# A decoder's fp8 self attention: the outputs' products in another accumulator bank, and the cross inputs' rounding at another place of the turn

## The chip, the core and the metric

The kernel is one program on one core of a Trainium2 chip. The metric is the device time of one execution in microseconds. A core has five engines that matter here, each with a queue of its own that it works through in order: TensorE (PE, matrix products, with a separate row PEld for loading its stationary operand), VectorE (DVE), ScalarE (ACT), GpSimd (POOL) and SyncE (SP, which issues nearly all DMAs). PE writes its products into eight accumulator banks (PSUM), from which DVE and ACT read them.

## What is computed

The reference is a two layer decoder on 16 sequences of 112 tokens with 512 channels. It runs in seven stages: a causal attention, an attention with fp8-rounded inputs (self and cross part), a mixture of experts, a second causal attention, a cross attention over the context, and a ternary feed-forward layer. The change lies in the self part of the second one:

```python
xq = _div_clamp_fp8(x, in_scale)          # clip to +-448, round to bf16, then to fp8 e4m3
q  = einsum('bsi,oi->bso', xq * in_scale, wq) * w_scale   # k and v alike, with scales of their own
p  = softmax(einsum('bsghd,btgd->bghst', ln(q), ln(k)) / sqrt(128))
o  = einsum('bghst,btgd->bsghd', p, v)    # then rounded to fp8 again, times wproj, added to x
```

The cross part needs the same x rounded with a fourth scale. The self stage does this rounding for it, on the side, and stores the result in DRAM.

## The kernel before

`stage_fp8_self` works on 64 units: a unit is one batch with one quarter q of the heads (four query heads, two key and value heads). Their order is fixed by `self_order`: quarters 0 and 1 are interleaved in units 0 to 31, then come quarter 2 (units 32 to 47) and quarter 3 (48 to 63). The 1792 tokens make 14 tiles of 128 rows, while a batch has 112 rows. So of eight batches, one (b = 7 or 15) has no tile of its own and hence no queries to project, and one (b = 0 or 8) finishes no tile and hence has no output product.

A software pipeline runs over turns: `turn(n)` issues one step each of several units. In the order of the code, and so of PE's queue, a turn holds the query product of unit n (`ps_q`), the scores of unit n-2 (`ps_s`), the transposes of the probabilities of unit n-3 (`ps_pt`), the key and value products of unit n (`ps_kv`), the values product of unit n-3 (`ps_av`), the transposes of queries and keys of unit n-1 (`ps_t`), and the output product of unit n-4 (`ps_acc`). PE and ACT keep the written order in all turns up to 63, DVE from turn 5 on. POOL and SP, and every engine in the last four turns (the drain), are ordered by the scheduler.

DVE's part of a turn, in order: the minimum over the scores (`su_m`), the sums of squares of the queries (`su_v`), the centring of new weights if any (`centers`), the reciprocals of the softmax sums (`su_s`), the second half of the weights' splitting (`ends`), the sums of squares of the keys, the smoothing and rounding of unit n-3's values (`smooth_fp8`, which uses `round_fp8`), the scaling of queries and keys (`qk`), the rounding of one cross tile (`quantize_cross`), and the addition of the output product to x (`x<-ps_acc`, in `add_output`). ACT computes the exponentials behind `su_m` (`pr`). POOL divides them by their sums (`pr<-pr,su_s`), subtracts weights' low halves (`w_self<-raw,w_self`), takes the power for the layer norm (`su_v`), and finishes each rounding (`r_o`, `xqx`).

`quantize_cross` runs in turns behind unit 31 in which no weights are centred, 14 times in all. It loads a tile `r_y` from `yx_dram`, rounds it with four DVE instructions (L530 to L534) and one on POOL (`xqx`), and stores it to `xx_dram`. The load and its rounding are in the same place of the same turn.

The stage divides the eight banks into pools: `mm` has three (for `ps_q` and `ps_kv`), `tr` one (for the transposes of the inputs, `ps_xt`, which end with the inputs in turn 20), `sc` four (for `ps_s`, `ps_pt`, `ps_av`, two `ps_t`, and `ps_acc`). The cross stage behind it has a bank `acc` for the same output products.

```python
tag = "acc" if "acc" in k.banks else "sc"
acc = k.psum.tile([P, D], F32, tag=tag, name="ps_acc", bufs=k.banks[tag])
```

Of the kernel before, what the change touches and what calls it, by code (L numbers as in the profile page):

```python
# [11 lines left out]
BF16 = mybir.dt.bfloat16  # L12
# [8 lines left out]
P = 128  # L21
# [4 lines left out]
KC = D // P  # L26
# [3 lines left out]
TILES = B * S // P  # L30
# [30 lines left out]
def done_tile(b):  # L61

    return tile_of(b - 1) if b % 8 else None
# [381 lines left out]
def from_positions(k, dst, src, t):  # L445

    src = src.rearrange("(s b) d -> b s d", b=B)
    for b, s, r, n in batches_of(t):
        k.nc.sync.dma_start(out=dst[r : r + n], in_=src[b, s : s + n])
# [73 lines left out]
def round_fp8(k, wk, y, parts, tag="r8"):  # L523

    nc = k.nc
    m = wk.tile(list(y.shape), BF16, tag=f"{tag}_m", name="r8_m", bufs=2)
    t = wk.tile(list(y.shape), BF16, tag=f"{tag}_t", name="r8_t", bufs=2)
    nc.vector.tensor_scalar(y, y, FP8_MAX, -FP8_MAX, ALU.min, ALU.max)  # L530
    nc.vector.tensor_scalar(m.bitcast(U16), y.bitcast(U16), 0x7F80, None, ALU.bitwise_and)
    nc.vector.tensor_scalar(m, m, 2.0**-6, 1.5 * 2.0**4, ALU.max, ALU.mult)

    nc.vector.tensor_tensor(t, y, m, ALU.add)  # L534
    for dst, tok in parts:
        nc.gpsimd.tensor_tensor(dst, t[:, :, tok], m[:, :, tok], ALU.subtract)  # L536
# [153 lines left out]
def two_parts(k, out, lhs, w, first=True, last=True):  # L690

    n = w[0].shape[1]
    for c in range(n):
        for i in range(2):
            k.nc.tensor.matmul(  # L695
                out, lhs(c), w[i][:, c, :], start=first and c == 0 and i == 0,
                stop=last and c == n - 1 and i == 1,
            )
# [55 lines left out]
def quantized(k, wk, b, xv):  # L754

    xq, t = None, tile_of(b)
    if t is not None:
        xq = wk.tile([P, 2, KC, P], F32R, tag="xq", name="xq", bufs=3)
        k.nc.sync.dma_start(out=xq.bitcast(F32), in_=k.xq_dram[t])
    xv[b] = wk.tile([P, KC, S], F32R, tag="xv", name="xv", bufs=4)  # L760
    k.last_load = k.nc.sync.dma_start(out=xv[b].bitcast(F32), in_=k.xv_dram[b])
    return xq


def quantize_cross(k, wk, t):

    y = wk.tile([P, KC, P], BF16, tag="r8_y", name="r8_y", bufs=2)
    k.nc.sync.dma_start(out=y, in_=k.yx_dram[t])
    xq = wk.tile([P, 2 * KC, P], BF16, tag="y_0", name="xqx", bufs=1)
    xq = xq.rearrange("p c s -> p (c s)").bitcast(F32).rearrange("p (c s) -> p c s", c=KC)  # L770
    round_fp8(k, wk, y, [(xq, slice(0, P))])
    k.nc.sync.dma_start(out=k.xx_dram[t], in_=xq)
# [10 lines left out]
class SelfUnit:  # L783
# [108 lines left out]
            )  # L892
        smooth_fp8(k, wk, av, 4 * self.q, self.b, self.heads.o)

    def output(self):
        t = done_tile(self.b)
        if t is not None:
            add_output(self.k, t, self.heads.o.pop(t), self.w.get(3))


def to_batches(k, wk, dst, ps, t, tag, cols):
# [20 lines left out]
    round_fp8(k, wk, y, parts)  # L922


def add_output(k, t, o, w):

    tag = "acc" if "acc" in k.banks else "sc"
    acc = k.psum.tile([P, D], F32, tag=tag, name="ps_acc", bufs=k.banks[tag])
    two_parts(k, acc, lambda h: o[:, h, :], w)
    x = k.x[:, t, :]  # L930
    k.nc.vector.scalar_tensor_tensor(x, acc, k.c_proj, x, ALU.mult, ALU.add)


def self_order():


    order, then = [], 0
    for b in range(B):
        order.append((0, b))
        while then < (b - 7) * 11 // 8:  # L940
            order.append((1, then))
            then += 1
    order += [(1, b) for b in range(then, B)]
    return order + [(q, b) for q in (2, 3) for b in range(B)]


def stage_fp8_self(k):

    nc = k.nc
    with k.stage("s2a", mm=3, tr=1, sc=4) as wk:
        order = self_order()
        total = len(order)
        heads, xv = [Heads() for _ in range(4)], [{} for _ in range(4)]
        units = [SelfUnit(k, wk, q, b, heads[q]) for q, b in order]
        inputs = {
            n: Quantized(k, wk, units[n].tile, xv[0])
            for n, (q, b) in enumerate(order) if q == 0 and units[n].tile is not None
        }  # L960
        weights = k.next_w + [Weights(k, "self", q, wk, raw=2) for q in (1, 2, 3)]
        weights.append(Weights(k, "cross", 0, wk, raw=2))
        last = [order.index((q, B - 1)) for q in range(4)]

        def at(n):
            return units[n] if 0 <= n < total else None


        early = {-2: 4, -1: 1, 0: 2, 1: 2, 2: 3, 3: 2, 4: 2}
        then = list(range(B))  # L970

        def products(count):
            for b in then[:count]:
                if b % GB == 2 and b // GB + 2 < NB:
                    k.early.load(b // GB + 2)
                k.early.product(b)
            del then[:count]

        def due(n):

            if n >= 3:
                yield weights[1], 2, 3
            for q in range(3):

                if n >= last[q]:
                    yield weights[q + 2], 2 if q == 0 else 1, 3 if n >= last[q] + 4 else 1 + (q < 2)

        tiles = list(range(TILES))

        def turn(n):  # L990
            new, half = inputs.get(n + 2), inputs.get(n + 1)
            products(early.get(n, 0))
            if at(n):
                units[n].project_q(weights[order[n][0]], xq.pop(n))
            if at(n - 2):
                units[n - 2].scores()
            if at(n):
                units[n].query_sums()
            if half:
                half.round_qk()  # L1000
                xq[n + 1] = half.xq
            centered = [w.centers() for w in weights]
            if at(n - 3):
                units[n - 3].transpose_probs()
            if at(n - 2):
                units[n - 2].exponentials()
            for w in weights:
                w.ends()
            if half:
                half.scale(6)  # L1010
            if at(n):
                units[n].project_kv(xv[order[n][0]].pop(order[n][1]))
            for w, count, pieces in due(n):
                w.begin(count, pieces)
            if at(n - 3):
                units[n - 3].values()
            if at(n):
                units[n].normalize()
            if half:
                half.round_v()  # L1020
            if n > last[1] and tiles and not any(centered):
                quantize_cross(k, wk, tiles.pop(0))
            if at(n - 1):
                units[n - 1].transpose()
            if new:
                new.transpose()
                new.scale(10)
            elif at(n + 2):
                q, b = order[n + 2]
                xq[n + 2] = quantized(k, wk, b, xv[q]) if q else None  # L1030
            if at(n - 4):
                units[n - 4].output()
            if n + 3 in inputs:
                inputs[n + 3].load()
            if 0 <= n < TILES:
                from_positions(k, k.x[:, n], k.x_dram, n)

        xq = {}
        inputs[0].load()
        fixed = {mybir.EngineType.PE, mybir.EngineType.Activation}  # L1040
        with k.tc.manual_schedule(engines=fixed):
            for n in range(-2, 5):
                turn(n)
        with k.tc.manual_schedule(engines=fixed | {mybir.EngineType.DVE}):
            for n in range(5, total):
                turn(n)
        for n in range(total, total + 4):
            turn(n)
        k.next_w = weights[-1]
# [10 lines left out]
class CrossUnit:  # L1060
# [111 lines left out]
    def output(self):  # L1172
        t = done_tile(self.b)
        if t is not None:
            add_output(self.k, t, self.heads.o.pop(t), self.w.get(1))


def stage_fp8_cross(k):
# [607 lines left out]
def stage_ffn(k):  # L1786
# [66 lines left out]

STAGES = (
    stage_attn0, stage_fp8_self, stage_fp8_cross, stage_moe, stage_attn1,
    stage_cross1, stage_ffn,
)
# [147 lines left out]
```

## Time and profile before

| | us |
|---|---|
| median of three runs | 3847.8 (3841.57 to 3852.76) |
| the profiled execution | 3842.72 |
| its span in the trace | 3841.0 |
| TensorE busy, granted clock over the span | 3627.2, 0.975 |
| self stage: rounding turns, first and second stretch | 695.4 to 785 and 828 to 867 |
| the four DVE instructions of one cross rounding | 0.29, 0.29, 0.29, 0.43 |
| POOL xqx, median | 1.158 |
| exponentials of one unit, chain of waits | 1.46 |
| x<-ps_acc on DVE, median | 0.745 |

A page shows one profiled execution. Where a row names a line such as L695, it is that of kernel.py. A count such as x14 says how often. In the view of waits a line has the waiting engine and instruction, then what it waited for, then the total, the number of waits and the longest in microseconds. In the timeline a row has its start, its duration, the engine, the line, what it writes and reads, and in square brackets how long the engine sat idle before it and who ended that.

### The profile page before, as it was taken

The numbers are of one execution on the slowest core, as the hardware profiler recorded it, in microseconds if no ns is written. First come the engines' busy times: TensorE is split into PE (matmuls) and PEld (weight loads), VectorE is DVE, ScalarE is ACT, GpSimd is POOL, SyncE is SP. The second block draws the span as 40 slices with busy tenths as digits, with TensorE's granted clock in tenths as the row PEclk, the third lists the DMA queues.
The fourth block names the chain that finished last, engine by engine and source line by source line (L and its number), as shares of the span: only waits on it lengthen the run. The fifth ranks groups of instructions, "written<-read, shape, count | busy, mean of one in ns | idle before, by whom it ended". The sixth has DMA issues, their size and how long they took to land.

```text
span 3841.0 us, 46297 instructions
## 1 busy us (share of the span) xinstructions
PE 3627.2 (94%) x16482; PEld 2338.3 (61%) x16482; DVE 1764.6 (46%) x3872; ACT 1437.4 (37%) x4149; POOL 926.1 (24%) x1314
## 2 busy tenths in 40 slices
PE   7888898899899999999999999999989999999999
PEld 4455787787555566656666654555544445556788
DVE  4445777776544544544445543111243343214333
ACT  2455675554444444444444430111123341112222
POOL 2333555553322322222222210000132220000000
PEclk8999899999999999999999999999989999999999
DMA  2125333432211211211121113999830022222000
GB/s 78 52 101 172 113 101 120 132 128 79 76 51 52 76 52 46 71 49 52 42 84 49 44 47 121 314 320 317 298 129 12 1 71 82 72 74 81 11 12 17
DMA packets 118117, 364.56 MB, mean 95 GB/s; under 512 B 13280, under 2 KB 33248, under 8 KB 108848
## 3 DMA queue, kind: packets, MB, share of 16 engines
q1 hardware_dynamic: 105504, 332.20, 26.7%
q0 software_dynamic: 5040, 16.52, 1.2%
q10 hardware_dynamic: 7344, 12.89, 0.9%
q8 instruction: 131, 2.15, 0.2%
q14 instruction: 98, 0.80, 0.1%
HBM read 317.09 MB, written 44.47 MB: 94 GB/s over the span
## 4 chain that ended last, share of the span: by engine, by line
PE 69%; DVE 8%; POOL 5%; DMA 3%; issue 2%; ACT 2%; SPq 0%; POOLq 0%; ACTq 0%; DVEq 0%
PE ps_kv L1113 14%; PE ps L1470 5%; PE ps_av L1166 4%; PE ps_s L1141 3%; PE ps_y L1488 3%; PE ps_q L695 3%; PE ps_acc L695 3%; PE ps_u L1832 3%; PE ps_o L350 3%; PE ps_o L1814 3%; PE ps_g L1832 3%; PE ps_q L1583 3%; PE ps_p L1676 3%; PE ps_pt L1156 2%; PE ps_v L1598 1%
## 5 line engine op out<-in xcount | busy, mean ns | idle before, releaser
L1113 PE MATMUL ps_kv<-w_kv,ct 128*125 128x512 f32 x1408 | 638.3, 593 | 0.0
L1113 PEld LDWEIGHTS ps_kv<-w_kv,ct 128*125 128x125 f32 x1408 | 260.5, 188 | 276.1 <-issue 242.0
L536 POOL TENSOR_TENSOR r_o<-r_t,r_m 128x64 fp32r<-128x64 bf16 (+6 forms) x224 | 146.6, 671 | 326.6 <-DVE r_t L534 302.9
L1057 ACT ACTIVATE pr<-ps_s,ex_m 112x375 f32<-112x375 f32 (+1 forms) x272 | 157.4, 579 | 164.6 <-DVE ex_m L1056 154.1
L1089 DVE TENSOR_REDUCE cu_v<-sq 125x2 f32<-125x256 f32 (+1 forms) x248 | 118.6, 478 | 217.5 <-ACT sq L1088 217.5
L1470 PE MATMUL ps<-w_expert,xgt 128*128 128x448 f32 x560 | 216.4, 539 | 0.7 <-ACT xgt L1462 0.7
L517 POOL TENSOR_SCALAR cu_v<-cu_v 125x2 f32<-125x2 f32 (+1 forms) x248 | 48.0, 194 | 635.9 <-DVE cu_v L1089 633.6
L236 POOL TENSOR_TENSOR pr<-pr,nq_s 112x448 f32<-112x448 f32 (+1 forms) x120 | 119.4, 996 | 320.2 <-DVE nq_s L235 266.0
L518 POOL TENSOR_TENSOR cu_v<-cu_v,mhalf 125x2 f32<-125x2 f32 (+1 forms) x248 | 190.0, 766 | 20.4
L231 ACT ACTIVATE pr<-ps_s,nq_m 112x112 f32<-112x112 f32 (+1 forms) x480 | 167.2, 376 | 52.5 <-DVE nq_m L223 48.6
L1141 PE MATMUL ps_s<-kt,qt 128*112 128x375 f32 x512 | 183.5, 479 | 1.7 <-ACT pr L1057 1.3
L1056 DVE TENSOR_REDUCE ex_m<-ps_s 112x1 f32<-112x375 f32 (+1 forms) x272 | 148.2, 545 | 69.1 <-PE ps_s L1703 68.0
L1088 ACT ACTIVATE sq<-ps_kv 125x256 f32<-125x256 f32 x176 | 67.4, 383 | 272.8 <-PE ps_kv L1113 218.5
L511 ACT ACTIVATE qt<-ps_t,turned 128x448 f32<-128x448 f32 (+6 forms) x224 | 116.5, 581 | 130.4 <-PE ps_t L1125 121.8
L1166 PE MATMUL ps_av<-pt,vn 125*128 125x224 f32 x768 | 160.8, 358 | 0.0
L1470 PEld LDWEIGHTS ps<-w_expert,xgt 128*128 128x128 f32 x560 | 103.6, 190 | 92.0 <-issue 91.0
L1156 PEld LDWEIGHTS ps_pt<-ident,pr 112*125 112x125 f32 x768 | 104.5, 190 | 86.3 <-DVE pr L1148 48.8
L1141 PEld LDWEIGHTS ps_s<-kt,qt 128*112 128x112 f32 x512 | 89.9, 177 | 100.8 <-issue 59.1
L245 ACT COPY ptt<-ps_pt 112x448 f32<-112x448 f32 (+1 forms) x120 | 66.8, 565 | 223.0 <-PE ps_pt L243 223.0
L1156 PE MATMUL ps_pt<-ident,pr 112*125 112x112 f32 x768 | 119.8, 285 | 30.9 <-DVE pr L1148 29.0
L1166 PEld LDWEIGHTS ps_av<-pt,vn 125*128 125x128 f32 x768 | 143.5, 192 | 8.7 <-ACT pt L1159 4.6
L511 ACT ACTIVATE kt<-ps_t,vec 128x375 f32<-128x375 f32 (+7 forms) x240 | 131.4, 588 | 26.0 <-PE ps_t L1131 22.0
(294 smaller groups left out, 7377.4 us busy)
## 6 DMA issues: line engine op xcount, KB each, us to landing
w_expert<-in_moe_w SPq DMA_DIRECT2D x105, 896.0 KB
ct<-in_ctx_t SPq DMA_DIRECT2D x64, 750.0 KB
xq<-xq_dram SPq DMA_DIRECT2D x42, 512.0 KB
xq<-xx_dram SPq DMA_DIRECT2D x56, 256.0 KB
raw<-in_self_w SPq DMA_DIRECT2D x48, 256.0 KB
w_sum<-in_ffn_w SPq DMA_DIRECT2D x12, 1024.0 KB
cn<-in_ctx SPq DMA_DIRECT2D x16, 750.0 KB
xv<-xv_dram SPq DMA_DIRECT2D x48, 224.0 KB
```

What stands on the lines that cost most here:

```text
L231: nc.scalar.activation(pr[:, j, :], self.ps[:, j, r * t : (r + 1) * t], AF.Exp, bias=self.mx[r][:, j : j + 1], scale=-1.0, accum_out=sums[ ...
L511: k.nc.scalar.activation(dst, src, AF.Identity, bias=cols[:, 1:2], scale=cols[:, 0:1])
L518: nc.gpsimd.tensor_tensor(dst, dst, bc(k.minus_half[: dst.shape[0]], [dst.shape[0], n]), ALU.pow)
L695: k.nc.tensor.matmul(out, lhs(c), w[i][:, c, :], start=first and c == 0 and i == 0, stop=last and c == n - 1 and i == 1,)
L1056: nc.vector.tensor_reduce(mx, src, AX.X, ALU.min)
L1057: nc.scalar.activation(dst, src, AF.Exp, bias=mx, scale=-1.0, accum_out=sums)
L1113: nc.tensor.matmul(pkv, self.ct[:, c, ch * CC : (ch + 1) * CC], w[:, c, :], start=c == 0, stop=c == KC - 1,)
L1141: nc.tensor.matmul(ps, self.heads.qt[self.b][:, h, :], self.kt[:, h // 2, :], start=True, stop=True)
L1156: nc.tensor.transpose(ps[:, h, :], self.pr[:, h, ch * CC : (ch + 1) * CC], k.ident[:S, :S])
L1166: nc.tensor.matmul(av[:, 2 * g : 2 * g + 2, :], self.vn[:, ch, g, :], self.pt[:, ch, 2 * g : 2 * g + 2, :], start=ch == 0, stop=ch == NCH - 1,
L1470: nc.tensor.matmul(pp, self.xt[:, c, :], w[:, c, :], start=c == 0, stop=c == 3)
L1832: nc.tensor.matmul(pp, w[:, c, cols], xt[:, part, c, :], start=c == 0 and part == 0, stop=c == 3 and part == 1,)
```

## The change

There are three edits.

1. `add_output` is told its bank by its caller. In the self stage this is `sc` up to the turn of the last input (turn 22), and `tr` from then on. The cross stage goes on using `acc`.
2. The load of a cross tile is a function of its own, `cross_input`. It stands where load and rounding stood, and is issued from turn 31 on whenever no loaded tile is pending. Its buffer is the one called `y_2`, which the inputs' values used before (one buffer), where `r_y` shared two with `smooth_fp8`.
3. The rounding of the tile loaded in the turn before stands behind `centers`, so on DVE behind `su_m` and the sums of the queries and ahead of `su_s`. On POOL its `xqx` then comes ahead of the same turn's `pr`. The turns in which a tile is rounded are the same 14.

```diff
-def quantize_cross(k, wk, t):
-
-    y = wk.tile([P, KC, P], BF16, tag="r8_y", name="r8_y", bufs=2)
+def cross_input(k, wk, t):
+
+    y = wk.tile([P, KC, P], BF16, tag="y_2", name="yx", bufs=1)
     k.nc.sync.dma_start(out=y, in_=k.yx_dram[t])
+    return y
+
+
+def quantize_cross(k, wk, t, y):
+
     xq = wk.tile([P, 2 * KC, P], BF16, tag="y_0", name="xqx", bufs=1)
...
-def add_output(k, t, o, w):
-
-    tag = "acc" if "acc" in k.banks else "sc"
+def add_output(k, t, o, w, tag):
+
     acc = k.psum.tile([P, D], F32, tag=tag, name="ps_acc", bufs=k.banks[tag])
...
-        tiles = list(range(TILES))
+        tiles, loaded = list(range(TILES)), []
+        end = max(inputs)
...
             centered = [w.centers() for w in weights]
+
+            if loaded and not any(centered):
+                quantize_cross(k, wk, *loaded.pop())
             if at(n - 3):
...
-            if n > last[1] and tiles and not any(centered):
-                quantize_cross(k, wk, tiles.pop(0))
+            if n >= last[1] and tiles and not loaded:
+                loaded.append((tiles[0], cross_input(k, wk, tiles.pop(0))))
...
-                units[n - 4].output()
+
+                units[n - 4].output("sc" if n <= end else "tr")
```

## The prediction

> **What bounds the kernel now.** First the page, to see which engine the program is against. TensorE is busy for 94% of the span.
>
> ```profile
> span 3841.0 us, 46297 instructions
> ...
> PE 3627.2 (94%) x16482; PEld 2338.3 (61%) x16482; DVE 1764.6 (46%) x3872; ACT 1437.4 (37%) x4149; POOL 926.1 (24%) x1314
> ```
>
> That is an average over seven stages. The change lives in one, the fp8 self attention, so second the table of busy time for its last part: the turns that round cross inputs (first and third row), those between them (second), and the rest.
>
> ```profile
> 695.40:785.00 89.60, 77.25 (x491) 67.99 (x490) 66.59 (x157) 47.23 (x159) 49.12 (x58) 0.98 0.44 144
> 785.00:828.00 43.00, 39.91 (x259) 35.06 (x258) 35.79 (x84) 25.00 (x81) 23.33 (x28) 1.00 0.37 119
> 828.00:867.00 39.00, 35.40 (x210) 31.60 (x211) 27.25 (x62) 18.63 (x62) 22.34 (x27) 0.87 0.35 112
> 867.00:934.00 67.00, 62.76 (x396) 55.15 (x395) 45.09 (x103) 36.05 (x127) 29.14 (x39) 1.00 0.22 70
> ```
>
> The columns are the length, then PE, PEld, DVE, ACT and POOL busy, and the granted clock. In the first row PE misses 12.4 us of 89.6; in the third it misses 3.6 and ran at a clock of 0.87. Third, who waits there (waits from 690 to 935):
>
> ```profile
> POOL pr L875 <- DVE su_s L874: 73.0, 26, 4.7
> ACT pr L870 <- POOL xqx L536: 23.8, 9, 4.1
> PEld ps_acc L695 <- issue: 12.3, 8, 1.9
> PE ps_acc L695 <- ACT pr L870: 10.0, 6, 1.7
> DVE r_y L530 <- DMA r_y<-yx_dram: 4.4, 8, 0.9
> ```
>
> The second line names POOL, but the built program makes those exponentials wait for su_m on VectorE; su_m ends at 724.13 and xqx at 724.19 in the same turn, so the view picked the later of two. Fourth, the chain of waits from 716 to 738, one turn:
>
> ```profile
> 718.64 2.87 DMA r_y<-yx_dram
> ...
> 723.02 1.17 POOL xqx L536
> 724.23 1.46 ACT pr L870 x8
> ...
> 726.04 0.93 POOL pr L875
> 726.97 1.25 POOL w_self L641
> ```
>
> and three rows of the timeline:
>
> ```profile
> 723.52 0.61 DVE L863 TENSOR_REDUCE su_m<-ps_s 112x4 f32<-112x448 f32 x1
> 725.78 2.09 PE L695 MATMUL ps_acc<-w_self,r_o 128*128 128x512 f32 x8 [1.59 <-ACT pr L870]
> ...
> 850.30 3.75 PE L695 MATMUL ps_acc<-w_self,r_o 128*128 128x512 f32 x8 [1.68 <-ACT pr L870]
> ```
>
> Read together this is a ring: load of r_y, rounding, x, su_m, exponentials, pr, the weights' low half on POOL, which frees raw for SP, which then issues the next r_y at 728.97. It turns once in 10.2 us (su_m at 713.50, 723.52, 733.73, 743.96), while PE without waits needs 8.17 (its scores at 873.00, 881.17, 889.34). The outputs' products hang on it, as their sc bank is the scores', which only the exponentials free.
>
> **The change, part by part.** I count turns as the code does; T38 starts with the su_m at 695.40. Rounding turns are T38 to T47 and T53 to T56, 14 of them. In the built program PE keeps its order up to the drain, ACT keeps it altogether; on DVE the four rounding instructions go from behind qk to behind su_m and the sums of q; on POOL xqx now comes ahead of pr in each turn.
>
> Load a turn ahead: same 14 DMAs on SP, each now behind its own turn's r_t, ahead of the xx store. It is issued about 2.6 us into a turn and wanted 1.1 us into the next one. Launch to use took 2.7 to 4.8 us; the room is over 6. So the DMA waits (4.4 us in 8) go. Behind the load on SP stand xx, raw, xv and xq; xq is for two turns later, raw still waits for POOL, so I cost this at nothing. Without that room each us of lateness would be a us of its turn, since su_s, pr and qk stand behind the rounding. The first load is issued in T31, eight turns early.
>
> Rounding behind su_m: a turn with weights on POOL (T40 to T43, T53, T54, T56) becomes: su_m start to rounding 1.14 (0.54 and 0.60 start to start), rounding 1.42, to xqx 0.07, xqx 1.17, so pr starts at 3.80 (it was 2.52: 723.52 to 726.04). From pr to qk stays 3.90 (726.04 to 729.94: pr, weights, the power), then qk to x 0.94 (872.01 to 872.95) and x to su_m 0.66. Sum 9.30 us. The exponentials (724.23 to 725.69, now from 0.71) lie beside the rounding. So the move takes the rounding and its DMA wait, about 2.2 us, off one side and puts 1.28 us on the other. In T40 to T43 that is 37.2 for 40.28 (10.02, 10.21, 10.23, 9.82).
>
> T38 and T39 (weights scaled on DVE; T39 has no queries): T38 without weights on POOL: pr ends 4.73, power to 6.40, 0.94 and 0.66: 8.00. T39 loses its trailing 1.35: 7.25 for 8.59. Together 15.25 for 18.10. T44 (no output) 7.35 for 7.38. T45 8.0, T46 8.0, T47 5.4 (su_m to su_s 2.19, the smoothing 2.5, x 0.66): 21.4 for 23.78. PE, from scores to scores 7.17 after a turn without queries and 6.3 in one, needs about 20.9 there and just fits. T53 9.30, T54 9.30, T55 5.85 (as T47, with weights on POOL): 24.45 for 29.44. T56 and T57 are then held by PE: 16.45 for 16.53.
>
> Outputs in tr: the waits of ps_acc on the exponentials go (about 1.7 each, eight of them; they lie inside the turns just summed), and one outside: at 638.95 ps_acc waited 1.68 in T31, and the next su_m waited 1.73 for PE behind it, so 1.7 more. What is new: tr has one buffer, so each product waits for the x before it. By the rows x ended at 873.69 and the next ps_acc began at 877.38, 3.7 us later; in the tight turns (T39, T47, T55) I find 0 to 0.2. [...] The rows put x in another part of the turn, so I take 0 in the turns. ps_t no longer waits for x (0.97 at 705.05, 1.92 at 848.18); that too is inside.
>
> Drain: there PE's order does change. Three of one output's matmuls stand ahead of a ps_av that waited 0.68 for pt, where PE was not the limit (0); one matmul stands ahead of the last ps_av and needs r_o, ready about 927.4, while that ps_av began at 926.82: 0.8 later. Bounds 0 and 0.8, I take 0.5.
>
> Clock: the row at 850.30 took 3.75 for 2.08, with the clock at 0.50 from 850 to 854, right behind waits of 1.92 and 1.68. [...] By the row I let it go with them. If it stays (2.4 us on PE), T55's end is PE's at 16.5 after T54's start and not 15.15: 1.35 dearer.
>
> Sum: T38 to T47 89.54 becomes 81.2, -8.3; T53 to T55 -5.0; T56 and T57 -0.1; T31 -1.7; drain +0.5; together -14.6 (by the clock rule -13.2). The profiled execution took 3842.7 (span 3841.0 and 1.7 around it), so it would take 3828. The three runs have a median of 3847.8, 5.1 above it; from there 3833.
>
> **The rivals.** *The gain is handed back on POOL.* pr now stands behind xqx. Against it: exponentials start 2 us earlier. For it: VectorE's rounding took 0.59 and 0.52 for 0.29 beside a POOL instruction (782.75), 0.53 more. In the seven turns with weights 9.3 becomes 9.8 and most of 4 us goes; with half of the waits in T31, T39, T47 and T55 replaced by PE's on qk or x, -7: 3841.
>
> *Slower: rounding between su_m and su_s.* Where a turn starts on PE's scores and not on DVE, earlier su_m is worth nothing, and each rounding turn pays 1.28 us on the path to pr, 14 x 1.28 = 18 us; less T31 and DMA waits it gives +12: 3860. It decides where scores come later than x. In T40 to T43 scores start about 6 us into the turn before and x ends at 9.3, so it does not; T45 and T46 are within 0.2 us of it.
>
> *The change doesn't do what it says*: the outputs' wait could be r_o, not the bank. r_o ended at 721.03 and ps_acc began at 725.78, right at the exponentials' end, so I give this nothing.
>
> **How the numbers follow.** Gain as summed (3827 to 3839): 0.60. Handed back (3837 to 3846): 0.27. Slower: 0.13. A measurement here tells about 0.3%, 11.5 us, from no change. Of the first case most lies beyond that bound (0.54); of the second nearly none (0.01). So faster 0.55, same 0.33, slower 0.12, as a little of the third case is within 0.3%. The range takes the first two cases, the bounds of drain and clock, and the start of the third: 3821 to 3853.
>
> **What would show it.** su_m to su_m should read about 9.3 in T40 to T43 and pr should start 3.8 after su_m; ps_acc should show no wait for pr; r_y's, now yx's, DMA wait should be gone; PE's clock in the third row should come near 1. T38 to T47 should last 81 us. I am wrong if xqx's start waits well past 2.7 us, if ps_acc waits for x, or if those turns stay near 10.

## The result, and the profile after

| | before | after |
|---|---|---|
| median of 12 runs each, us | 3848.14 | 3833.39 |
| ratio, with its 95% interval | | 0.9958 (0.9945 to 0.9970) |
| the profiled execution, us | 3842.72 | 3829.97 |
| span, us | 3841.0 | 3828.2 |

The changed kernel is faster by 0.42% (14.75 us by the medians, 12.75 by the profiled executions). The prediction said 14.6. The page first:

```profile
span 3828.2 us, 46333 instructions
...
PE 3624.2 (95%) x16482; PEld 2336.8 (61%) x16482; DVE 1772.0 (46%) x3872; ACT 1437.1 (38%) x4149; POOL 927.7 (24%) x1314
```

TensorE did the same work in nearly the same busy time, so the gain is waiting that went. The table of the self stage's last part, cut at the same turns as before (length, then PE, PEld, DVE, ACT and POOL busy, granted clock, DMA share, GB/s):

```profile
693.37:775.11 81.74, 76.21 (x488) 67.61 (x488) 71.90 (x156) 47.32 (x159) 49.20 (x57) 0.98 0.49 161
775.11:818.19 43.08, 40.19 (x261) 35.35 (x260) 35.88 (x85) 25.00 (x81) 23.39 (x29) 1.00 0.35 113
818.19:852.74 34.55, 31.29 (x198) 27.14 (x198) 30.51 (x61) 18.50 (x62) 22.81 (x27) 0.99 0.40 130
852.74:920.85 68.11, 64.18 (x405) 56.99 (x404) 44.11 (x102) 36.37 (x127) 28.62 (x38) 0.98 0.21 65
```

The first row is T38 to T47: PE now misses 5.5 us of 81.7 where it missed 12.4 of 89.6. The clock of the third row came from 0.87 to 0.99, but that of the last fell from 1.00 to 0.98: a spell at half clock now lies there, from 852 to 855, around the start of T57. Read turn by turn (from one su_m to the next):

| turns | before | after | predicted |
|---|---|---|---|
| T31 | 7.02 | 5.21 | 5.3 |
| T38, T39 | 9.51, 8.59 | 8.93, 7.07 | 8.00, 7.25 |
| T40 to T43 | 10.02, 10.21, 10.23, 9.82 | 9.34, 9.22, 9.23, 9.23 | 9.30 each |
| T44 to T47 | 7.38, 8.08, 8.49, 7.21 | 7.29, 7.94, 7.94, 5.55 | 7.35, 8.0, 8.0, 5.4 |
| T53, T54, T55 | 10.17, 9.85, 9.42 | 9.22, 9.21, 6.78 | 9.30, 9.30, 5.85 |
| T56 + T57 | 16.53 | 18.08 | 16.45 |
| T31 to T57, with the turns between | 237.29 | 224.96 | |

The turns give 12.3 of the 12.8 us of span; of the rest, 0.3 is lost again from T58 to the cross stage's first `ps_q`, and 0.8 is gained elsewhere in the span. Of that 0.3 is the bank's, in T24, the turn behind the first product in `tr`: 7.02 before, 6.71 with the bank, 7.04 in e2 without it. The other 0.5 has no cause that the runs show. What now waits for what, in the waits from 680 to 921 of the changed kernel:

```profile
POOL pr L880 <- DVE su_s L879: 56.2, 15, 4.7
POOL xqx L536 <- DVE su_s L879: 30.8, 11, 3.2
ACT pr L875 <- DVE su_m L868: 28.8, 19, 3.4
...
PE ps_kv L695 <- DVE qk L840: 9.4, 8, 2.2
...
PE ps_acc L695 <- POOL r_o L536: 3.3, 4, 1.6
```

Three things are to be seen. VectorE's wait for the DMA of the cross tile and `ps_acc`'s wait for the exponentials are gone. `ps_acc` does not wait for x either, with its single buffer. And PE waits for `qk` instead, at the end of the chain through POOL. One turn of that chain (start, length, engine and what):

```profile
718.79 0.53 DVE su_m L868
719.32 0.59 DVE su_v L800
719.91 0.21 DVE yx L530
...
720.80 0.43 DVE r_t L534
721.23 0.10 DVE su_s L879
721.33 0.04 POOL xqx L536
...
722.42 0.93 POOL pr L880
723.35 1.25 POOL w_self L641
724.61 0.21 POOL su_v L517
...
724.89 1.42 POOL su_v L518
...
726.33 1.02 DVE qk L840 x2
727.35 0.66 DVE x L935
728.01 0.53 DVE su_m L868
```

There is no DMA in this ring any more: it is VectorE, POOL and VectorE again, 9.22 us long. The gap from 721.33 to 722.42 is `pr` standing behind `xqx` on POOL, 1.1 us in which it has its sums already. PE alone would need 8.17.

### The profile page after: what moved, and what is told of

It is laid out like the page before. It is cut to its first block, busy times and chain, and to the rows that moved or that the text cites. A ratio compares the mean times of both kernels' runs of the same rounds, so it can differ in the third digit from the quotient of the medians.

```text
span 3828.2 us, 46333 instructions
## 1 busy us (share of the span) xinstructions
PE 3624.2 (95%) x16482; PEld 2336.8 (61%) x16482; DVE 1772.0 (46%) x3872; ACT 1437.1 (38%) x4149; POOL 927.7 (24%) x1314
## 3 DMA queue, kind: packets, MB, share of 16 engines
q8 instruction: 131, 2.15, 0.2%
## 4 chain that ended last, share of the span: by engine, by line
PE 68%; DVE 10%; POOL 5%; issue 2%; DMA 2%; ACT 2%; SPq 0%; POOLq 0%; ACTq 0%; DVEq 0%
PE ps_kv L1122 14%; PE ps L1479 6%; PE ps_av L1175 4%; PE ps_s L1150 3%; PE ps_y L1497 3%; PE ps_u L1841 3%; PE ps_q L695 3%; PE ps_acc L695 3%; PE ps_o L350 3%; PE ps_g L1841 3%; PE ps_o L1823 3%; PE ps_q L1592 3%; PE ps_pt L1165 2%; PE ps_p L1685 2%; PE ps L1431 2%
```

## The experiments

Below, "W turns" are T40 to T43, those with weights' low halves on POOL. All turn lengths are from each kernel's own trace, that is from one profiled execution. The changed kernel was profiled twice, and T38 to T55 agree within 0.01 us in the two (e9 below). Of the single edits e1 and e3 have ratios whose intervals include 1, and that of e2 ends at 0.9998, so what each edit is worth is read from the turns and not from the times.

| | T31 | T38 to T47 | of these W turns, mean | T53 to T57 |
|---|---|---|---|---|
| before | 7.02 | 89.54 | 10.07 | 45.97 |
| changed kernel | 5.21 | 81.74 | 9.26 | 43.29 |
| e1 bank alone | 5.21 | 90.02 | 10.13 | 44.27 |
| e6 own buffer alone | 9.89 | 86.28 | 9.40 | 43.82 |
| e3 bank, buffer, load ahead | 5.21 | 86.07 | 9.36 | 43.13 |
| e2 all but the bank | 8.59 | 83.28 | 9.26 | 43.65 |
| e5 all, load in its own turn | 5.21 | 81.76 | 9.26 | 43.45 |
| e4 all, xqx behind r_o | 5.21 | 76.28 | 8.45 | 39.26 |
| e7 all, xqx ahead of r_o | 5.21 | 76.87 | 8.31 | 39.80 |

### e1: the bank alone

```diff
-    y = wk.tile([P, KC, P], BF16, tag="y_2", name="yx", bufs=1)
+    y = wk.tile([P, KC, P], BF16, tag="r8_y", name="r8_y", bufs=2)
...
-            if loaded and not any(centered):
-                quantize_cross(k, wk, *loaded.pop())
...
-            if n >= last[1] and tiles and not loaded:
-                loaded.append((tiles[0], cross_input(k, wk, tiles.pop(0))))
+            if n > last[1] and tiles and not any(centered):
+                t = tiles.pop(0)
+                quantize_cross(k, wk, t, cross_input(k, wk, t))
```

(The diffs of e1 to e5, e7 and e8 are against the changed kernel, that of e6 against the kernel before.)

> Only the first edit: outputs' products in tr after turn 22, load and rounding of the cross tile as before. Theory (the ring through rounding, pr and the power sets the turns, and the products only hang on it): T40 to T43 stay at 10.0 to 10.2, T31 goes from 7.02 to 5.3, the turns without queries (T39, T47, T55) give up to 1 each; together -4 (-2 to -7), about 3844. Rival (the outputs' bank is what carries the gain): T40 to T43 fall to about 9.3 and the time to 3836 or less.

Median 3843.79, ratio to before 0.9995 (0.9983 to 1.0007). T31 fell to 5.21 as expected and the W turns did not move (9.79, 10.33, 10.55, 9.83): the bank does not carry the gain there. T39 and T47 stayed at 8.59 and 7.21, T55 gave 1; from T31 to T57 it is 2.8 us, within the 2 to 7 expected. And there is a wait that neither of the two profiles above has:

```profile
PE ps_acc L695 <- DVE x L935: 3.6, 3, 2.0
```

With the rounding between `qk` and x, x comes late, and the next product stands in front of the one buffer of `tr`. The longest is in T55 (PE's timeline, idle time in brackets; the product itself took 3.65 for 2.08, at half clock):

```profile
843.94 3.65 PE L695 MATMUL ps_acc<-w_self,r_o 128*128 128x512 f32 x8 [2.03 <-DVE x L935]
```

So the single buffer brings waits of its own, though T39, T47 and T55 are no longer than before for them: those turns end on VectorE here. The changed kernel has no such wait, because the rounding no longer stands ahead of x.

### e2: everything but the bank

```diff
-                units[n - 4].output("sc" if n <= end else "tr")
+                units[n - 4].output("sc")
```

> The second and third edit alone: load a turn ahead, rounding behind the minimum, outputs' products in sc as before. Theory: T40 to T43 at 9.2 to 9.3 as in the changed kernel, since there ps_acc begins 3 to 4 us into the turn, behind the exponentials' end at 2.2; T31 back at 7.0; the turns without queries up to 1 dearer each; together -10 (-8 to -12), about 3838. Rival (the bank carries it): T40 to T43 near 10 and the time within 3 us of before.

Median 3840.41, ratio 0.9984 (0.9969 to 0.9998). The W turns are those of the changed kernel, so there the bank is worth nothing. It is worth 1.5 in T47 (7.04 for 5.55), more than the "up to 1" expected, and nothing in T39 (7.08 for 7.07). T55 is 1.8 longer without it (8.61 for 6.78), but most of that is a spell at half clock: the product took 3.65 for 2.08, and the next su_m waited 1.74 for PE. At full clock about 0.3 would be left (an estimate, 1.83 less 1.57). T31 was not 7.0 but 8.59; its `ps_acc`, behind the same wait of 1.68 for the exponentials as before, ran at half clock too:

```profile
641.21 3.40 PE L695 MATMUL ps_acc<-w_self,r_o 128*128 128x512 f32 x8 [1.68 <-ACT pr L875]
...
846.36 3.65 PE L695 MATMUL ps_acc<-w_self,r_o 128*128 128x512 f32 x8 [1.24 <-issue]
```

### e3: the rounding back between qk and x

```diff
-            if loaded and not any(centered):
-                quantize_cross(k, wk, *loaded.pop())
...
+            if loaded and not any(centered):
+                quantize_cross(k, wk, *loaded.pop())
             if n >= last[1] and tiles and not loaded:
```

> Bank and load a turn ahead as in the changed kernel, the rounding back between qk and x. Theory: a turn with weights on POOL is pr at 2.5, to qk 3.9, rounding and x 0.94 + 1.35, to su_m 0.66: 9.3 to 9.5, so most of the gain in T40 to T43 comes from the load, and the place of the rounding only trades 1.3 on one side for 1.2 on the other; T31 at 5.2; together -9 (-6 to -12), about 3839. Rival (the place of the rounding is what matters): T40 to T43 stay near 10.0 and the gain is under 5.

Median 3839.62, ratio 0.9985 (0.9966 to 1.0005). The W turns are at 9.33 to 9.39, as the theory had it: moving the rounding is worth 0.1 in such a turn. It is worth 0.5 in T38, 1.5 in T39 (8.59 for 7.07), 1.65 in T47 (7.20 for 5.55) and 1.65 in T55 (8.43 for 6.78). These last three have no queries. In T39, T47 and T55 `ps_acc` waits for x again:

```profile
PE ps_acc L695 <- DVE x L935: 3.7, 5, 1.3
```

T47 shows how the edits lean on each other: 7.21 before, 7.21 with the bank, 7.20 with bank and load, 7.04 with load and place, and 5.55 with all. Two ways of nearly the same length led to that turn's end: VectorE through rounding and x, and PE through `ps_acc`, `ps_q` and the scores. Shortening one shows only when the other is short too.

### e5 and e6: which part of the second edit does it

e5 has all of the change but the turn of lead in the code:

```diff
-            if loaded and not any(centered):
-                quantize_cross(k, wk, *loaded.pop())
+            if n > last[1] and tiles and not any(centered):
+                t = tiles.pop(0)
+                quantize_cross(k, wk, t, cross_input(k, wk, t))
...
-            if n >= last[1] and tiles and not loaded:
-                loaded.append((tiles[0], cross_input(k, wk, tiles.pop(0))))
```

> Bank, yx's own buffer and the rounding behind the minimum as in the changed kernel, but the load is written in the same turn, right ahead of its rounding. SP's queue is ordered by the scheduler, and in the built program it holds the loads in the same places as in the changed kernel, as a load needs only its buffer. Theory (what the load needs is a free buffer and its place in SP's queue, not its place in the code): T40 to T43 at 9.2 to 9.3, no wait of VectorE for yx. Rival (the turn of lead in the code is what hides the transfer): a wait for yx of 1 to 3 us in each rounding turn, T40 to T43 at 10.5 or more.

One run, 3831.92. T38 to T47 are at 81.76, turn by turn within 0.02 of the changed kernel. The lead in the code does nothing: SP's queue is ordered by the scheduler, and it holds the loads in the same order as in the changed kernel.

e6 has the buffer alone, in the kernel before:

```diff
-    y = wk.tile([P, KC, P], BF16, tag="r8_y", name="r8_y", bufs=2)
+    y = wk.tile([P, KC, P], BF16, tag="y_2", name="yx", bufs=1)
     k.nc.sync.dma_start(out=y, in_=k.yx_dram[t])
```

> The kernel before with one edit: the cross tile is loaded into yx's own buffer (y_2) and no longer into one of the two that smooth_fp8 uses; load and rounding stand in the same turn behind qk, outputs in sc. In SP's queue the load still stands behind raw. Theory (the load is late because it stands behind raw, which waits for POOL's low halves): T40 to T43 stay at 10.0 to 10.2 with waits for yx of 0.5 to 0.9. Rival (the shared buffer delayed it): T40 to T43 fall to 9.4 as in the run with bank and load alone.

One run, 3842.49, with half clock in T31 (9.89), T39 and T55. Here my theory fell: the W turns went to 9.35 to 9.51, and VectorE's wait for the tile is gone. SP's queue in the timeline says why. First the kernel before, then e6 (start, length, queue, line, what):

```profile
718.22 0.33 SPq L629 DMA_DIRECT2D raw<-in_self_w  x1
718.64 0.38 SPq L768 DMA_DIRECT2D r_y<-yx_dram  x1
...
728.25 0.33 SPq L629 DMA_DIRECT2D raw<-in_self_w  x1
728.97 0.32 SPq L768 DMA_DIRECT2D r_y<-yx_dram  x1
```

```profile
718.53 0.33 SPq L629 DMA_DIRECT2D raw<-in_self_w  x1
...
722.63 0.32 SPq L768 DMA_DIRECT2D yx<-yx_dram  x1
...
727.91 0.33 SPq L629 DMA_DIRECT2D raw<-in_self_w  x1
```

In both the load follows a `raw`. But in the kernel before it is launched right behind it and used in the same turn (rounded at 721.53). In e6 the load launched at 722.63, as soon as the rounding of the tile before it has let go of the buffer, is the one that is rounded at 730.55. So it is a whole turn ahead, with no line of code moved. I had read that the load "stands behind raw" off the order of names, and overlooked that it was another tile's load. Why the scheduler holds the load back when the buffers are shared with `smooth_fp8` was not tried.

### e4 and e7: xqx out of pr's way

e4 splits the rounding. VectorE's four instructions stay behind su_m, POOL's `xqx` and the store come behind the turn's `values()`, and POOL keeps the written order from turn 32 on.

```diff
-                quantize_cross(k, wk, *loaded.pop())
+                finish = quantize_cross(k, wk, *loaded.pop())
...
             if at(n - 3):
                 units[n - 3].values()
+            if finish:
+                finish()
             if at(n):
                 units[n].normalize()
...
-            for n in range(5, total):
+            for n in range(5, last[1] + 1):
                 turn(n)
+        with k.tc.manual_schedule(engines=fixed | {mybir.EngineType.DVE, mybir.EngineType.Pool}):
+            for n in range(last[1] + 1, total):
+                turn(n)
```

> As the changed kernel, but POOL in the written order from turn 32 on, with xqx behind the turn's last r_o and not ahead of pr; DVE's, PE's and ACT's order as in the changed kernel. Theory (in the changed kernel pr waits 1.1 to 1.2 behind xqx in each turn with weights on POOL): pr starts 2.6 after su_m and not 3.7, T40 to T43, T53 and T54 go from 9.2 to 8.2, where PE holds them; PE's waits of 2.1 on qk and with them the two spells at half clock go; -6 to -9 against the changed kernel, about 3826. Rival (VectorE, slowed beside POOL, is the next bound): the turns stay at 8.8 or more and the time within 3 us of the changed kernel.

Median 3826.43, ratio to before 0.9941 (0.9928 to 0.9954). On POOL's queue nothing but `xqx` stands elsewhere than in the changed kernel, on SP's its store comes later and a few loads change places, and on VectorE's nothing moves. POOL and su_m in one W turn of e4:

```profile
721.39 0.61 DVE L875 TENSOR_REDUCE su_m<-ps_s 112x4 f32<-112x448 f32 x1
...
724.22 0.93 POOL L887 TENSOR_TENSOR pr<-pr,su_s 112x448 f32<-112x448 f32 x1 [2.19 <-PE ps_t L862]
725.11 1.29 POOL L642 TENSOR_TENSOR w_self<-raw,w_self 128x512 fp32r<-128x512 f32 x1
...
728.07 1.17 POOL L536 TENSOR_TENSOR r_o<-r_t,r_m 128x384 fp32r<-128x384 bf16 x2
...
729.21 1.16 POOL L781 TENSOR_TENSOR xqx<-r_t,r_m 128x512 f32<-128x512 bf16 x1
729.73 0.62 DVE L875 TENSOR_REDUCE su_m<-ps_s 112x4 f32<-112x448 f32 x1
```

`pr` starts 2.83 after su_m where it started 3.71, and the turn takes 8.34 where it took 9.22. T41 to T43, T53 and T54 lie at 8.24 to 8.34, against PE's 8.17; T40 took 8.89, behind a T39 that is 0.4 shorter (6.67 for 7.07). PE's row over T38 to T47 says that it is the bound again:

```profile
697.88:774.16 76.28, 74.08 (x488) 66.17 (x488) 66.37 (x156) 47.30 (x159) 49.14 (x58) 1.00 0.52 169
```

It misses 2.2 us of 76.3, at full clock.

e7 has the `finish()` ahead of `values()`, so that `xqx` is ahead of `r_o` and behind the power.

> As the run with xqx behind the turn's last r_o, but xqx ahead of r_o and still behind the power. r_o comes 1.2 later in each rounding turn. Theory (pr's place behind xqx was the cost, and r_o has over 2 us of room before ps_acc in these turns): T40 to T43 at 8.2 to 8.9, the time within 2 us of that run, 3824 to 3829. Rival (r_o is the next limit): ps_acc waits 0.5 to 1 for r_o in turns with weights on POOL and these turns take 8.8 or more.

Median 3827.47, ratio 0.9939 (0.9900 to 0.9978). The same within what the medians tell. T38 to T47 came to 76.87 for 76.28; T39 and T55 are 1.1 dearer (7.79 and 7.63), and the turns behind them 0.6 cheaper. `ps_acc` waits for `r_o` in total 3.3 in four places, as in e4 and the changed kernel: `r_o` has its room.

### e8: the drain

```diff
-                units[n - 4].output("sc" if n <= end else "tr")
+                units[n - 4].output("sc" if n <= end or n >= total else "tr")
```

(this on top of e4)

> As the run with xqx behind r_o, and the outputs of the four last turns again in sc; TensorE's order in the drain is then that of the kernel before. From the last full turn's scores to the cross stage's first ps_q it should take 0.3 to 0.8 less than in that run; the time is the same within 2 us. Rival (the bank costs nothing in the drain): the same to 0.1.

Median 3829.74, ratio 0.9958 (0.9933 to 0.9983): that is 3.3 above e4's 3826.43, where the same within 2 was expected; medians of five runs tell nothing about half a microsecond. The traces do. From the start of the last scores but one to that of the cross stage's first `ps_q` it takes 17.30 us in the kernel before, 17.82 in the changed one, 17.83 in e4 and 17.29 in e8. So the bank costs 0.53 in the drain, in each of these.

### e9 and e10: changed kernel and e4 on the same chip

> The changed kernel, beside the version with xqx behind r_o on the same chip. Its turns T38 to T47 at 81.7, T53 to T57 at 43.3 where a spell at half clock falls behind PE's wait for qk in T56 and 41.5 where not; 3831 to 3836.

> The version with xqx behind the turn's last r_o. If its turns (76.3 for T38 to T47, 39.3 for T53 to T57) carry over to the time, it is 6 to 9 below the changed kernel of the same call, 3824 to 3828. Rival (the difference of the two earlier calls was chance): within 3 us of it.

Medians 3835.15 and 3826.64; ratios to the same runs of before 0.9967 (0.9942 to 0.9993) and 0.9948 (0.9932 to 0.9964). Of the 8.5 us between the medians the turns give 7.9 (T31 to T57: 223.60 and 215.69), though the intervals of the two ratios overlap. In e9 T56 and T57 took 9.34 and 7.22, with no spell of half clock behind the wait in T56.

## Why the prediction was right, point by point

**The ring and its end.** T40 to T43, T53 and T54 were to take 9.30 and took 9.21 to 9.34; `pr` was to start 3.80 after su_m and started 3.71. The way through su_m, rounding, `xqx`, `pr`, the low half, the power, `qk` and x was the right one.

**What I credited for it was not right.** The working let the move of the rounding take 2.2 us (with the DMA wait) off one side and put 1.28 on the other. e6 and e3 split this: 0.7 of a W turn is the DMA wait, which goes with the buffer alone, and the move itself is worth 0.1. The turn of lead, which the prediction took for what hides the transfer ("launch to use took 2.7 to 4.8 us; the room is over 6"), is worth nothing in the code (e5). Nor is the ring's way from the weights' low half through `raw` to the next load needed for the wait: e6 leaves `raw` where it was, behind the low half, and the wait is gone. The sum held because the wait and the move were counted together.

**Where the gain is.** Adding the edits in the order e6, e3, changed kernel gives, by T38 to T47 and T53 to T57 together: own buffer 5.4 us, bank and lead 0.9 (and 1.8 in T31), the rounding's place 4.2, or 5.7 by e9, which has no spell in T57. The place pays most in the turns without queries, where the way through PE is short: in T39 with or without the bank (7.07 and 7.08), in T47 only with it (5.55, and 7.04 without).

**T38 and T55, 0.9 too short each.** This is the step whose size was wrong: durations of VectorE's instructions were taken without what runs on POOL at the time. In T55 one mask of the rounding of the outputs took 2.05 us for 0.28:

```profile
840.03 2.05 DVE L531 TENSOR_SCALAR r_m<-r_y 128x448 uint16<-128x448 uint16 x1
```

POOL's `pr` ran from 839.75 to 840.72 and its `w_cross` from 840.68 to 841.95: the mask ended 0.13 behind the second of them. The profile before has such a row in the same turn, which the prediction does not mention; it ended 0.13 behind POOL's `w_cross`, which ran from 851.45 to 852.73:

```profile
850.96 1.90 DVE L530 TENSOR_SCALAR r_y<-r_y 128x448 bf16<-128x448 bf16 x1
```

In T38 the two splittings of weights (L646) took 2.54 beside `xqx` and `pr`, and 1.56 in e4, beside `pr` alone; T38 fell from 8.93 to 7.95, which is this difference. Why VectorE's instructions took longer beside POOL's, the rows do not show. The rival "handed back on POOL" had this cost, at 0.5 a turn, but put it in the turns with weights on POOL. There it is hidden, since VectorE waits for POOL's power anyway (L530 took 1.71 at 723.03, `qk` still waited 0.47 for the power, and the turn still took 9.22).

**The half clock, a term that went the other way.** I let the spell at 850 to 854 go with the waits before it, and it went. Another came behind the new wait for `qk`:

```profile
851.89 2.08 PE L695 MATMUL ps_kv<-w_self,xq 128*128 128x256 f32 x8 [2.15 <-DVE qk L840]
853.76 1.76 PE L695 MATMUL ps_kv<-w_self,xv 128*112 128x256 f32 x8
```

The granted clock reads 0.50 from 852 to 855. T56 and T57 took 18.08 for the 16.45 predicted. In e9, the same kernel without the spell, they took 16.56, so this term was right without it and 1.5 short with it. No run shows the rule that the prediction's other value, -13.2 "by the clock rule", is named after; what the changed kernel showed in its place is half clock behind windows of 3.41 us of which PE was busy for 1.24 and 1.33 (last section). That value was the nearer one for this execution, which gained 12.75, but by luck: it let the old spell stay in T55, and that one went.

**The bank.** T31 was to give 1.7 and gave 1.8; the drain was to cost 0.5 and cost 0.53. That x would not hold up the products was right for the changed kernel, which has no such wait, and for the reason given ("x in another part of the turn"): where the rounding stands ahead of x, as in e1 and e3, the products wait 3.6 and 3.7 us in all.

**The total.** The errors in the turns (0.9 + 0.9 + 1.5, less small gains in and outside the turns) leave the profiled execution 2 us above the 3828 that the sum gave for it. That the median came out at 3833.4 where 3833 stood is chance to this extent. The rival "slower" did not come: scores were never later than x in T40 to T43, and T45 and T46, the two within 0.2 us of it, took 7.94.

## What to carry to other kernels

Here a wait for a load was cured by a buffer of its own sooner than by an earlier line, as the queue that issues it is ordered by a scheduler: compare which transfer feeds which use in the trace, not the order of names. When a piece of side work moves along one engine, look at where its second half lands on the next engine: here four instructions on VectorE cost nothing at their new place, while one on POOL, 1.1 us ahead of the softmax's division, was worth 7 to 8.5 us once it stood behind the power. Two ways of nearly equal length into the same turn need both edits before either shows.

## What the runs showed of the hardware that was not expected

The length of one wait of PE did not decide whether half clock followed. The same schedule has a wait of 2.15 to 2.18 us at the end of T40 and of T56. At T40 a spell of 3 to 4 us followed in the changed kernel and e9 but not in e5, and at T56 in the changed kernel and e5 but not in e9. In e6 a spell fell on a wait of 1.68 in T39 (`ps_acc` at 707.33 took 3.66), where the kernel before had the same wait and none (707.17, 2.08). What differed is where the wait fell. In all twelve traces the granted clock changes only on a grid of 3.41 us, and this grid lies elsewhere in each execution. The traces cut at it:

| | window of the grid | PE busy in it, us | clock in the next |
|---|---|---|---|
| changed kernel, wait at the end of T40 | 715.28 to 718.69 | 1.24 | 0.50 |
| e5, the same wait | 713.87 to 717.28 | 2.36 | 1.00 |
| | 717.28 to 720.69 | 2.28 | 1.00 |
| changed kernel, wait at the end of T56 | 848.40 to 851.81 | 1.33 | 0.50 |
| e9, the same wait | 849.95 to 853.36 | 2.38 | 1.00 |
| | 853.36 to 856.77 | 2.28 | 1.00 |
| e6, wait in T39 | 703.93 to 707.35 | 0.82 | 0.50 |
| before, the same wait | 705.31 to 708.72 | 1.73 | 1.00 |

A wait of about 2.17 that lay in one window was followed by half clock in both rows that have it (PE was busy for 1.24 and 1.33 us of the window), and the same wait split over two was not in either (2.28 to 2.38 in each window). In T39 of e6 a second wait (0.92 for x) lies in the same window. From 560 to 945 us of the twelve traces, the next window ran at half clock behind all 24 full-clock windows in which PE was idle for over 2.1 us, behind 16 of 37 with 1.6 to 2.1, and behind none of over a thousand with less. Over the whole traces the bounds are less sharp (223 of 269 above 2.1, and 16 cases between 1.3 and 1.6).

In e4, e7, e8 and e10 the only wait over 1.35 us in T38 to T57 is one of 1.40 to 1.98 each, and no spell showed in any of the four.

What a spell cost was not the same in each turn. In T57, where PE was busy throughout and the next su_m waited 1.58 for it, it cost 1.5 us (8.74, and 7.22 in e9); the one behind T40, where the next su_m did not wait for PE, cost nothing (T40 and T41 took 9.34 and 9.22 with it, 9.35 and 9.23 in e5 without). A part of what a removed wait is worth here is thus the spell that it may bring, and whether it brought one changed from one execution to the next.
